# A graph network on one core: ScalarE's instructions tied to the order in which the kernel writes them

## Chip, core and metric

The kernel runs on one core of a Trainium2 chip. The metric is the time of one execution on the device in microseconds (us), the median of three runs. One further execution was recorded by the hardware profiler; all durations below come from its trace.

## What is computed

Three layers of a graph network (SAGE), each the sum of a node's own row and the mean of its neighbours' rows, through two weight matrices; then a residual and a layer norm; then one attention layer over the same edges, again with residual and layer norm. There are 12,500 nodes with 256 features, and 200,000 edges sorted by their target node.

```
def _sage_layer(x, src, dst, inv_deg, W_self, W_neigh, b):
    agg = jax.ops.segment_sum(x[src], dst, num_segments=N_NODES)
    mean = agg * inv_deg[:, None]
    return x @ W_self + mean @ W_neigh + b
...
h = jax.nn.relu(_sage_layer(features, ...)); h = jax.nn.relu(_sage_layer(h, ...)); h = _sage_layer(h, ...)
x = _layernorm(x + h)
x = _layernorm(x + attention(x))
```

## The kernel before

The neighbour sums of a layer are made in two ways at once. The edges of the lower nodes are taken in groups of 1,792 (14 columns of 128): layer 0 has 90 groups, layers 1 and 2 have 76 each. For each group GpSimd fetches 14 times 128 source rows (`gather`, line 121) into one of three buffers `xg`. From the middle of layer 0 on, ScalarE rounds the rows to a short format (line 858, tile `hl` or `win`), VectorE makes the rest (line 860), and TensorE multiplies them with a one-hot matrix of the targets into `pA` (lines 866, 869, 874). The nodes behind them (20 blocks of 128 in layer 0, 32 in the others) are summed densely: a matrix of edge counts in bytes, built in layer 0 (`form`, lines 615 to 652: VectorE makes two one-hots, TensorE multiplies them into `pc`, ScalarE packs `pc` into `win` at line 645), is multiplied with the whole table of rows (`sweeps`, lines 687 to 770). For each block of 128 table rows ScalarE turns a tile of counts into `c32` (line 749; 512 columns in layer 0, 1,024 in the others; three buffers), and TensorE runs four or eight matmuls of 128x512 on it (line 755). Such a block is called a sweep step here.

Each group also has an end. ScalarE copies half of the sum (`part`, line 904, then VectorE adds at 905) and scales it to `mean` (908); in layer 0 it copies the sum to `agg` (910). TensorE turns the rows (363) and makes eight weight products into `pO` (354). VectorE adds the bias in place (344). In layers 0 and 1 ScalarE then makes `hn` (346) and `hs` (659) with Relu; in layer 2 VectorE adds `x` (348) and takes statistics (334, 335), ScalarE takes the root `bn_rs` (337), and a later projection `zu` (376) is squared by ScalarE (`sq`, 672). The dense blocks end in the same way, with `own` (720), `hnd` (346) and `hs` (`end_block`, line 698).

The kernel's loop over groups (lines 928 to 957) writes the steps of three groups and of the sweeps in a fixed interleaving, `turns`. On TensorE that order is binding: `chained` ties the first matmul of each step behind the last one of the step before, without a semaphore. GpSimd's gathers are tied in the same way, and `hold_back` paces them. All other engines' orders are chosen when the kernel is built: a scheduler places an instruction where it expects its inputs to be there. On each engine the placed order is kept at run time.

Of the kernel before, what the change touches and what calls it, by code (L numbers as in the profile page):

```python
# [23 lines left out]
P = 128  # L24
# [15 lines left out]
CB = 7  # L40
# [8 lines left out]
def tile_gnn_resnorm(  # L49
# [70 lines left out]
    def gather(dst_ap, table, idx):  # L120
        return nc.gpsimd.indirect_dma_start(  # L121
            out=dst_ap, out_offset=None, in_=table,
            in_offset=bass.IndirectOffsetOnAxis(ap=idx, axis=0))


    src0 = const.tile([P, G0, GT], I32, name="src0")
# [61 lines left out]
    with tc.tile_pool(name="prep", bufs=1) as prep, \  # L188
# [126 lines left out]
        hex_ = prep.tile([KR, K], F32, name="hex_")  # L315
        nc.scalar.activation(hex_, hw, AF.Exp, bias=hmx)
        hsum = prep.tile([KR, 1], F32, name="hsum")
# [11 lines left out]
    def layernorm(wk, y, o):  # L329

        n = y.shape[0]
        st = wk.tile([n, nc.vector.BN_STATS_DIM], F32, name="bn_st")
        mv = wk.tile([n, nc.vector.BN_AGGR_DIM], F32, name="bn_mv")
        nc.vector.bn_stats(st, y)
        nc.vector.bn_aggr(mv, st)
        rs = wk.tile([n, 1], F32, name="bn_rs")
        nc.scalar.activation(rs, mv[:, 1:2], AF.Sqrt, bias=eps_t[:n])
        nc.vector.reciprocal(rs, rs)
        return nc.vector.tensor_scalar(o, y, mv[:, 0:1], rs, op0=OP.subtract, op1=OP.mult)

    def sage_end(wk, l, wts, po, hn, xb):

        n = po.shape[0]
        nc.vector.tensor_add(po, wts[2][:n], po)
        if l < L - 1:
            return nc.scalar.activation(hn, po, AF.Relu)
        y = wk.tile([n, D], F32, name="y")
        nc.vector.tensor_add(y, xb, po)
        return layernorm(wk, y, hn)
# [8 lines left out]
    def turned(wk, ps, tiles, name, bufs=None, by_act=False):  # L358
# [6 lines left out]
        if by_act:  # L365
            nc.scalar.activation(t, pt, AF.Copy)
        else:
            nc.vector.tensor_copy(t, pt)
# [28 lines left out]
    def attention_turned(wk, pt, n):  # L397
        agT = wk.tile([KR, n], F32, name="agT")
        nc.scalar.activation(agT, pt[:KR], AF.Copy)
        return agT  # L400

    def attention_end(wk, zz, pg):

        n = zz.shape[0]
        g = wk.tile([n, D], F32, name="g")
        nc.scalar.activation(g, pg, AF.Relu, bias=shrink[:n])
        nc.vector.tensor_add(g, zz, g)
        return g, layernorm(wk, g, g)
# [3 lines left out]

    DATA = mybir.DependencyReason.DATA
    AFTER = mybir.DependencyInfo(mybir.DependencyClass.NoSync, DATA)
    DONE = mybir.DependencyInfo(mybir.DependencyClass.Sync, DATA)
    loads = [None]
# [25 lines left out]
    def hold_back(first, then):  # L442

        tc.add_manual_dep(then.ins, first.ins.name, DONE, reason="the pace of the gathers")

    def after(first, then):

        tc.add_manual_dep(then.ins, first.ins.name, AFTER, reason="the order of the work")

# [21 lines left out]
    def fast_sage():  # L471
        with ExitStack() as fx:
# [7 lines left out]
            ones2 = wp.tile([P, 2], F32R, name="ones2")  # L480
            nc.scalar.activation(ones2, ones[:, :2], AF.Copy)
            invd = wp.tile([P, ND], F32, name="invd")
# [8 lines left out]
            for a in range(0, NG * GT, P):  # L491
# [3 lines left out]
                rt = wk.tile([P, P], F32, name="rt")  # L495
                nc.scalar.activation(rt[:m], pr[:m], AF.Copy)
                nc.sync.dma_start(rel_d[a:a + m, :], rt[:m])
# [10 lines left out]
            def split_x(pool, psum):  # L508
# [13 lines left out]
                for b in range(0, NQ, ZB):  # L522
# [5 lines left out]
                    for n, r in ((P, slice(0, m)), (N % P, slice(m, ZB))):  # L528
                        if r.start == r.stop:
                            continue  # L530
                        hi = hs[:n, r, :D]
                        nc.scalar.activation(hi.bitcast(F32R), xv[:n, r], AF.Copy)
                        nc.scalar.activation(ph[:n, r], hi, AF.Copy)
                        nc.vector.tensor_tensor(hs[:n, r, D:].bitcast(F32R), xv[:n, r], ph[:n, r], op=OP.subtract)
# [33 lines left out]
            def load_edges(pool, u):  # L568
# [41 lines left out]
                for i in range(3):  # L610
                    nc.tensor.transpose(pt[:, i], keys[:, i], ident)
                nc.scalar.activation(kt, pt, AF.Copy)
                held.append(kt)

            def form(pool, psum):
# [6 lines left out]
                for i, u in enumerate(parts):  # L622
# [3 lines left out]
                    for i0 in range(0, P, CP):  # L626
# [9 lines left out]
                        for c in range(0, CP, 2):  # L636
                            d = (i0 + c) * NC % P
                            if d == 0:
# [5 lines left out]
                            chained(*mm)  # L644
                            nc.scalar.activation(  # L645
                                win[:, :, d:d + 2 * NC].bitcast(U16).rearrange("p b (i t) -> p b i t", t=2),
# [8 lines left out]
            def finish(l, lk, bank, hn, po, last=False):  # L655

                if l < L - 1:
                    hs = lk.tile([P, 2 * D], F32R, name="hs", bufs=3)
                    nc.scalar.activation(hs[:, :D], po, AF.Relu)
                    hf = hs.bitcast(F32)  # L660
# [10 lines left out]
                sq = lk.tile([P, KR], F32, name="sq")  # L671
                nc.scalar.activation(sq, zu, AF.Square)
                nrm = lk.tile([P, K], F32, name="nrm")
# [13 lines left out]
            def sweeps(l, dk, dps, lk):  # L687
# [10 lines left out]
                def end_block(k, d, aggT, bank):  # L698
# [20 lines left out]
                    own = wk.tile([P, D], F32, name="own", bufs=1)  # L719
                    nc.scalar.activation(own, po, AF.Copy)  # L720
                    nc.vector.scalar_tensor_tensor(po, pn, invd[:, k + d:k + d + 1], own, op0=OP.mult, op1=OP.add)
# [16 lines left out]
                for k0 in range(ND - NDL[l], ND, sg):  # L738
                    assert all(k in whole for k in range(k0, k0 + sg))
                    px = [[dps.tile([P, 512], F32, name=f"px{f}{i}") for i in range(sc // 512)] for f in range(DC)]  # L740
                    for b in range(NQ):
# [6 lines left out]
                        c32 = dk.tile([P, sc], F32R, name="c32", bufs=3)  # L748
                        nc.scalar.activation(c32.rearrange("p (k d) -> p k d", d=P), c8[:, :, b % CB], AF.Copy)  # L749
                        made = []  # L750
# [14 lines left out]
                    for f in range(DC):  # L765
                        for i in range(sc // 512):
                            nc.scalar.activation(aggT[:, f, i * 512:(i + 1) * 512], px[f][i], AF.Copy)
                    left = end_sweep(k0, aggT, [ps])
# [30 lines left out]

            turn, H, summed = 0, GT // 2, []  # L800
            for l in range(L):
                table = x if l == 0 else hd[l - 1]
# [5 lines left out]
                with ExitStack() as lx:  # L808
# [11 lines left out]
                    def group(g):  # L820
# [28 lines left out]
                        for a in (0, H):  # L849
# [4 lines left out]
                            if halved:  # L854
                                hf = hi.bitcast(F32)
                                for j in range(0, H, 2):
                                    n = min(2, H - j)
                                    nc.scalar.activation(hi[:, b + j:b + j + n, :W], xg[:, a + j:a + j + n, :W], AF.Copy)  # L858
                                for j in range(H):
# [42 lines left out]
                        if l:  # L902
                            part = wk.tile([P, D], F32, name="part")
                            nc.scalar.activation(part, pa[:, D:], AF.Copy)
                            nc.vector.tensor_add(before[:, :D], part, pa[:, :D])
                        sums = before[:, :D] if l else pa[:, :D]
                        mean = wk.tile([P, D], F32, name="mean", bufs=3)
                        nc.scalar.activation(mean, sums, AF.Copy, scale=inv[:, g:g + 1])
                        if not l:
                            nc.scalar.activation(before[:, :W], pa[:, :W], AF.Copy)  # L910
                        yield
# [47 lines left out]
                    assert next(steps_, None) is None and (l or (next(forming, 0) == 0 and next(xsplit, 0) == 0))  # L959

            t1 = wp.tile([P, 1], F32, name="t1")
            nc.vector.reduce_max(t1, top, axis=AX.X)
# [6 lines left out]
    def fast_attention():  # L969
        loads[0] = None  # L970
        H = GT // 2
        with tc.tile_pool(name="att", bufs=2) as wk, \
# [11 lines left out]
            def group(g):  # L984
# [20 lines left out]
                oT = ohT[:, :T].rearrange("p j e -> p (j e)")  # L1005
                nc.scalar.activation(oT, rT, AF.Abs, bias=npidx)
                nc.scalar.activation(oT, rT, AF.Relu, scale=-1.0, bias=1.0)

                z2 = wk.tile([P, K, 2, R], F32R, name="z2", bufs=3)
                zk = zn.rearrange("p (k r) -> p k r", r=R)  # L1010
                nc.scalar.activation(z2[:, :, 0], zk, AF.Copy)
                nc.vector.tensor_tensor(z2[:, :, 1], zk, z2.bitcast(F32)[:, :, 0], op=OP.subtract)

                w = wk.tile([P, GT, 2 * AW], F32R, name="w", bufs=3)
                for a, n in ((0, H), (H, T - H)):
# [4 lines left out]
                          for j in range(n)]  # L1020
# [10 lines left out]
                    wf = wk.tile([P, H, AW], F32, name="wf")[:, :n]  # L1031
                    nc.scalar.activation(wf[:, :, KR:], lg, AF.Exp, scale=0.25)  # L1032
                    pe = pd[:, H * 2 * KR:H * 2 * KR + n * K].rearrange("p (t k) -> p t k", k=K)
                    nc.scalar.activation(pe, wf[:, :, KR:], AF.Copy)
                    nc.vector.tensor_mul(wf[:, :, :KR].rearrange("p t (k r) -> p t k r", r=R),  # L1035
                                         zs[:, a:a + n].rearrange("p t (k r) -> p t k r", r=R),
                                         pe.unsqueeze(3).to_broadcast([P, n, K, R]))
                    nc.scalar.activation(w[:, a:a + n, :AW], wf, AF.Copy)
                    nc.vector.tensor_tensor(w[:, a:a + n, AW:], wf, w.bitcast(F32)[:, a:a + n, :AW], op=OP.subtract)
# [9 lines left out]
                part = wk.tile([P, AW], F32, name="part")  # L1049
                nc.scalar.activation(part, pa[:, AW:2 * AW], AF.Copy)  # L1050
                acc = wk.tile([P, AW], F32, name="acc", bufs=3)
# [86 lines left out]
    def general_sage():  # L1138
        for l in range(L):
# [16 lines left out]
            with tc.tile_pool(name="gn", bufs=1) as wk, tc.tile_pool(name="gn_ps", bufs=1, space=PSUM) as ps:  # L1156
                wts = load_sage(wk, l)
                with tc.For_i(0, NBLK, 1) as i:
# [13 lines left out]
                    mean = wk.tile([NB, D], F32, name="mean")  # L1172
                    nc.scalar.activation(mean, ab[:, :D], AF.Copy, scale=iv)
                    po = sage_products(ps, wts, turned(wk, ps, [hb, mean], "hT")[0])[0]
# [12 lines left out]
    def general_attention():  # L1187
# [20 lines left out]
        with tc.tile_pool(name="gs", bufs=1) as wk, tc.tile_pool(name="gs_ps", bufs=1, space=PSUM) as ps:  # L1208
            with tc.For_i(0, NTE, 1) as i:
# [8 lines left out]
                w = wk.tile([TE, AW], F32, name="w")  # L1218
                nc.scalar.activation(w[:, KR:], lg, AF.Exp)
                nc.vector.tensor_mul(w[:, :KR].rearrange("p (k r) -> p k r", r=R),  # L1220
# [63 lines left out]
```

## Time and profile before

| | us |
|---|---|
| median of the three runs | 8058.46 |
| lowest and highest run | 8031.01 and 8086.6 |
| the profiled execution's own time | 6504.63 |
| its span, first to last instruction | 6502.8 |
| TensorE busy in the span | 5140.6 |
| GpSimd busy | 4809.5 |
| VectorE busy | 3906.3 |
| ScalarE busy | 3473.9 |

The first gather of layer 1 starts at 1705.5 us of the span, the first load that only layer 2 makes at 3105.2 us, and the attention's matmuls start at 4502.8 us. The layers thus take about 70 to 4480 us, and the attention some 2,020 us. The profiled execution is shorter than the runs by 1,554 us; no record of the runs says where they take longer. The mean granted clock of TensorE in the profiled execution is 0.815 of full speed. In the profile's rows PE is TensorE's matmuls, PEld its weight loads, DVE VectorE, ACT ScalarE, POOL GpSimd and SP the engine that issues most transfers.

### The profile page before, as it was taken

What the parts mean: (1) busy time and instruction counts of PE and PEld (TensorE: products, weight loads), DVE (VectorE), ACT (ScalarE), POOL (GpSimd) and SP (SyncE); (2) the same over time, 40 slices, a digit from 0 to 9 for tenths busy, and PEclk for the clock granted to TensorE, in tenths of its full rate; (3) what the DMA queues carried; (4) which work ended last, traced back from release to release, by engine and by line L of the source; (5) the groups of instructions that cost most, each with busy time, mean ns of one, the idle gap of its engine ahead of it and who ended that gap; (6) DMA issues with size and microseconds to landing.
All of it is one profiled execution on the core that took longest, in us unless ns stands there. A gap on an engine that the chain in (4) does not pass through costs nothing.

```text
span 6502.8 us, 86803 instructions
## 1 busy us (share of the span) xinstructions
PE 5140.6 (79%) x23570; PEld 4209.6 (65%) x23570; DVE 3906.3 (60%) x9939; ACT 3473.9 (53%) x6309; POOL 4809.5 (74%) x4977
## 2 busy tenths in 40 slices
PE   4789999888799999998899999995555555555555
PEld 3567777677577777786678888884444444444444
DVE  4867767555445555555456666665555655556555
ACT  2444555565466666664556666664454554545554
POOL 6767777777677777776777777776777777777775
PEclk8889999999899999998899999997555555555555
DMA  8978999898678888886788888885333333333332
GB/s 219 319 259 291 305 305 320 284 302 289 189 254 260 267 267 270 261 273 197 230 264 265 272 269 273 271 246 149 93 107 102 101 101 102 105 105 101 101 101 73
DMA packets 896774, 1391.65 MB, mean 214 GB/s; under 512 B 191216, under 2 KB 540424, under 8 KB 892173
## 3 DMA queue, kind: packets, MB, share of 16 engines
q1 hardware_dynamic: 650511, 834.50, 38.8%
q0 software_dynamic: 213152, 496.65, 26.9%
q10 hardware_dynamic: 32606, 54.81, 2.4%
q8 instruction: 189, 3.10, 0.2%
q14 instruction: 316, 2.59, 0.1%
HBM read 1175.15 MB, written 210.33 MB: 213 GB/s over the span
## 4 chain that ended last, share of the span: by engine, by line
PE 25%; POOL 10%; DMA 7%; DVE 5%; issue 5%; ACT 1%; DVEq 0%; POOLq 0%; SPq 0%; ACTq 0%
POOL zs L121 9%; PE px L755 9%; DMA zs<-zu_d,srcI 4%; PE pA L866 3%; DMA xg<-h_d,srcI 3%; PE pA L1042 3%; PE pD L1018 3%; PE pO L381 2%; PE pO L354 2%; PE pO L382 1%; DVE wf L1035 1%; DVE zz L1026 1%; DVE lg L1029 1%; PE pT L363 1%; PE pA L469 1%
## 5 line engine op out<-in xcount | busy, mean ns | idle before, releaser
L121 POOL DMA_INDIRECT xg<-h_d,srcI x2128 | 2076.2, 976 | 704.1 <-issue 288.6
L755 PE MATMUL px<-c,hz 128*128 128x512 f32 x8232 | 2255.5, 414 | 110.0 <-ACT c L749 83.5
L121 POOL DMA_INDIRECT zs<-zu_d,srcI x1563 | 1499.1, 959 | 505.5 <-issue 425.4
L755 PEld LDWEIGHTS px<-c,hz 128*128 128x128 f32 x8232 | 1521.7, 191 | 427.8 <-ACT c L749 107.1
L121 POOL DMA_INDIRECT xg<-in_x_dram,srcI x1218 | 1172.4, 963 | 426.9 <-issue 136.9
L749 ACT ACTIVATE c<-c 128x1024 fp32r<-128x1024 uint8 (+1 forms) x1274 | 1120.1, 892 | 598.7 <-PE px L755 424.3
L860 DVE TENSOR_TENSOR hl<-xg,hl 128x256 fp32r<-128x256 f32 x2128 | 790.1, 419 | 578.5 <-ACT hl L858 575.4
L858 ACT ACTIVATE hl<-xg 128x512 fp32r<-128x512 f32 x1216 | 648.6, 571 | 612.9 <-DMA xg<-h_d,srcI 484.5
L462 DVE TENSOR_TENSOR oh<-rel,gconst 128x1792 fp32r<-128x1792 f32 (+1 forms) x354 | 713.8, 2017 | 334.2 <-PE pA L866 193.1
L1056 PE MATMUL pT<-ident,ag 128*64 128x128 f32 x112 | 47.1, 421 | 887.5 <-DVE ag L392 887.5
L1056 PEld LDWEIGHTS pT<-ident,ag 128*64 128x64 f32 x112 | 14.4, 129 | 967.4 <-DVE ag L392 966.1
L1026 DVE TENSOR_TENSOR zz<-zs,pD 128x896 f32<-128x896 f32 x224 | 241.9, 1080 | 636.6 <-DMA zs<-zu_d,srcI 632.5
L866 PE MATMUL pA<-hl,oh 128*128 128x512 f32 x2128 | 574.7, 409 | 12.8 <-DVE hl L860 9.2
L866 PEld LDWEIGHTS pA<-hl,oh 128*128 128x128 f32 x2128 | 406.3, 193 | 108.5 <-DVE hl L860 13.8
L874 PE MATMUL pA<-xg,oh 128*128 128x258 f32 x1764 | 431.4, 397 | 6.1 <-ACT agg L910 3.4
L1018 PE MATMUL pD<-z,ohT 128*128 128x128 f32 x1563 | 360.7, 418 | 39.0 <-DVE wf L1035 21.9
L874 PEld LDWEIGHTS pA<-xg,oh 128*128 128x128 f32 x1764 | 343.7, 199 | 64.0 <-ACT agg L910 7.2
L645 ACT ACTIVATE win<-pc 128x392 uint16<-128x392 f32 x512 | 238.5, 494 | 272.3 <-PE pc L642 263.4
L1018 PEld LDWEIGHTS pD<-z,ohT 128*128 128x128 f32 x1563 | 346.8, 333 | 39.7 <-DVE wf L1035 22.2
L1042 PE MATMUL pA<-w,oh 128*128 128x136 f32 x1563 | 361.3, 418 | 0.0
L1032 ACT ACTIVATE wf<-lg 128x28 f32<-128x28 f32 x224 | 50.5, 226 | 576.4 <-DVE lg L1029 575.2
L634 DVE TENSOR_SCALAR ob<-iota,kt 128x196 bf16<-128x196 f16 x1024 | 349.7, 344 | 0.0
(257 smaller groups left out, 7879.8 us busy)
## 6 DMA issues: line engine op xcount, KB each, us to landing
hz<-hs_d SPq DMA_DIRECT2D x637, 512.0 KB
c<-cnt_d SPq DMA_DIRECT2D x112, 896.0 KB
ohT<-rel_d SPq DMA_DIRECT2D x111, 896.0 KB
hs_d<-hs SPq DMA_DIRECT2D x218, 256.0 KB
cnt_d<-win ACTq DMA_DIRECT2D x32, 1568.0 KB
xg<-h_d,srcI POOLq DMA_INDIRECT x2128
c<-cnt_d SPq DMA_DIRECT2D x70, 448.0 KB
zs<-zu_d,srcI POOLq DMA_INDIRECT x1563
```

The source lines that it names most:

```text
L121: return nc.gpsimd.indirect_dma_start(out=dst_ap, out_offset=None, in_=table, in_offset=bass.IndirectOffsetOnAxis(ap=idx, axis=0))
L462: nc.vector.tensor_tensor(oh[:, :m], r[:, :m].unsqueeze(2).to_broadcast([P, m, P]), nodes.unsqueeze(1).to_broadcast([P, m, P]), op=op)
L634: nc.vector.tensor_scalar(ob[:, c], iota16[:, 1:1 + NQ * 2], kt[:, 1, at], kt[:, 2, at], op0=OP.is_equal, op1=OP.mult)
L749: nc.scalar.activation(c32.rearrange("p (k d) -> p k d", d=P), c8[:, :, b % CB], AF.Copy)
L755: made.append(nc.tensor.matmul(px[f][i], hz[:, b % ZB, a:a + P].bitcast(F32R), c32[:, i * 512:(i + 1) * 512], start=b == 0 and part == 0, ...
L858: nc.scalar.activation(hi[:, b + j:b + j + n, :W], xg[:, a + j:a + j + n, :W], AF.Copy)
L860: nc.vector.tensor_tensor(lo[:, b + j, :D], xg[:, a + j, :D], hf[:, b + j, :D], op=OP.subtract)
L866: mm.append(nc.tensor.matmul(pa, oh[:, a + j], hl[:, j].rearrange("p i d -> p (i d)"), start=first, stop=stop))
L874: mm.append(nc.tensor.matmul(pa[:, :W], oh[:, a + j], xg[:, a + j, :W], start=first, stop=stop))
L1018: mm = [nc.tensor.matmul(pd[:, j * 2 * KR:(j + 1) * 2 * KR], ohT[:, a + j], z2.rearrange("p k i r -> p (k i r)"), start=True, stop=True) f ...
L1026: nc.vector.tensor_mul(zz, zg.unsqueeze(2).to_broadcast([P, n * K, 2, R]), pd[:, :n * 2 * KR].rearrange("p (m i r) -> p m i r", i=2, r=R))
L1042: mm = [nc.tensor.matmul(pa, oh[:, j], w[:, j], start=j == 0, stop=g == 0 and j == T - 1) for j in range(T)]
```

## The change

A wrapper `act` takes the place of `nc.scalar.activation` everywhere in the fast path. While a switch is on, which is from the first line of the loop over layers to its end, each activation is tied behind the one written ahead of it. The tie is the same that `chained` uses: a place in the engine's own order, with no semaphore. The transfers that ScalarE issues are not tied, nor are activations before the layers and in the attention. No instruction is added or taken away.

```
     DATA = mybir.DependencyReason.DATA
     AFTER = mybir.DependencyInfo(mybir.DependencyClass.NoSync, DATA)
     DONE = mybir.DependencyInfo(mybir.DependencyClass.Sync, DATA)

     def after(first, then):

         tc.add_manual_dep(then.ins, first.ins.name, AFTER, reason="the order of the work")

+    written = [False, None]
+
+    def act(*args, **kw):
+
+        i = nc.scalar.activation(*args, **kw)
+        if written[0]:
+            if written[1] is not None:
+                after(written[1], i)
+            written[1] = i
+        return i
...
-            return nc.scalar.activation(hn, po, AF.Relu)
+            return act(hn, po, AF.Relu)
...
-                        nc.scalar.activation(c32.rearrange("p (k d) -> p k d", d=P), c8[:, :, b % CB], AF.Copy)
+                        act(c32.rearrange("p (k d) -> p k d", d=P), c8[:, :, b % CB], AF.Copy)
...
             turn, H, summed = 0, GT // 2, []
+            written[0] = True
             for l in range(L):
...
+            written[0] = False
             t1 = wp.tile([P, 1], F32, name="t1")
```

The lines left out replace the other calls in the same way; `DATA`, `AFTER`, `DONE` and `after` only move up.

## Prediction

> **What bounds the kernel now.** I read the engines' totals first, then the stages, then the rows of single instructions, the waits and the timeline. First three stages (columns: busy us of PE, PEld, DVE, ACT, POOL, granted clock, DMA share, GB/s): the middle of layer 1, the start of layer 2, its middle; then two stretches of 20 us in layer 0.
>
> ```profile
> 2500.00:2900.00 400.00, 386.25 (x1727) 316.72 (x1726) 216.34 (x496) 258.79 (x434) 304.60 (x314) 0.99 0.83 267
> 3100.00:3500.00 400.00, 371.19 (x1669) 300.24 (x1669) 230.96 (x602) 232.73 (x385) 304.29 (x315) 0.97 0.81 254
> 3500.00:4000.00 500.00, 499.97 (x2381) 412.67 (x2380) 339.02 (x930) 307.26 (x525) 381.12 (x391) 1.00 0.87 271
> ...
> 600.00:620.00 20.00, 15.81 (x86) 11.78 (x85) 15.88 (x67) 8.36 (x20) 14.95 (x17) 0.91 0.80 260
> 1360.00:1380.00 20.00, 15.83 (x83) 12.85 (x82) 11.31 (x30) 12.59 (x28) 15.27 (x16) 0.99 0.88 292
> ```
>
> TensorE has no free time in layer 2's middle and 3 to 7% elsewhere in mid-layer. Summed over the stages from 70 to 4480 us it idles 369 us: 198 in the four stages that hold the starts and ends of layers, 172 in between. GpSimd is close behind: a gather takes 0.95 us and the pause after it 0.30, so 14 cost 17.5 us, against 18.0 to 18.4 us for a group (1,620 us / 90; 1,395 / 76; 1,380 / 76). ScalarE is busy for 60% only: its work doesn't matter, its places do.
>
> TensorE around a group's weight products in layer 2, and ScalarE at that time:
>
> ```profile
> 3806.74 1.03 PE L354 MATMUL pO<-ws,hT 128*128 128x256 f32 x4
> 3807.61 1.03 PE L354 MATMUL pO<-wn,hT 128*128 128x256 f32 x4
> 3808.29 2.19 PE L755 MATMUL px<-c,hz 128*128 128x512 f32 x8
> 3810.32 0.38 PE L363 MATMUL pT<-ident,hn 128*128 128x128 f32 x2
> 3810.45 2.09 PE L755 MATMUL px<-c,hz 128*128 128x512 f32 x8
> ```
> ```profile
> 3804.45 0.63 ACT L858 ACTIVATE hl<-xg 128x512 fp32r<-128x512 f32 x1 [0.51 <-PE pA L866]
> ...
> 3806.79 1.06 ACT L749 ACTIVATE c<-c 128x1024 fp32r<-128x1024 uint8 x1
> 3807.75 0.49 ACT L908 ACTIVATE mean<-agg,inv 128x256 f32<-128x256 f32 x1
> 3810.57 1.06 ACT L749 ACTIVATE c<-c 128x1024 fp32r<-128x1024 uint8 x1 [2.32 <-issue]
> 3811.53 0.28 ACT L337 ACTIVATE bn_rs<-bn_mv,eps_t 128x1 f32<-128x1 f32 x1
> ```
>
> TensorE goes from the products straight into the next sweep steps, since ScalarE had cast their counts (`c`) before it comes to the root (`bn_rs`) that depends on those products. Only few waits of TensorE on ScalarE are left (us in total, times, longest):
>
> ```profile
> PE px L755 <- ACT c L749: 83.5, 37, 6.9
> PE pc L642 <- ACT win L645: 47.7, 16, 17.6
> ...
> ACT hl L858 <- DMA xg<-h_d,srcI: 484.5, 293, 11.0
> ```
>
> **The change, part by part.** Nothing is added or removed; I compared the two built orders. In longest common order, 4180 of ScalarE's 6514 instructions keep their places, 21082 of TensorE's 22197, 5114 of GpSimd's 5127, 4609 of SP's 5016, 7820 of VectorE's 10126. So ScalarE changes, TensorE hardly, and VectorE follows ScalarE. Neither the gathers nor SP's loads move far (at most 28 and 40 places), and their number is the same; I cost them at nothing as GpSimd has no harder bound than before. If a load came late, a sweep step (2.0 us) waits for it.
>
> What matters is what stands behind an activation that waits. As written, a group's end reads: products on TensorE; `hn`, `hs` (or `bn_rs`) on ScalarE; then the next sweep step's cast and its matmuls. A layer 0 example from the new orders:
>
> ```
> ScalarE: hn_8051<-pO_8046, hs_8054<-pO_8046, c32_8064, win_7957<-pc_8070, c32_8074
> TensorE: pO_8046 (products), px<-c32_8064 (x4), pc_8070 (x2), px<-c32_8074 (x4)
> ```
>
> `c32_8064` cannot start before `hn` has had the products, and TensorE has nothing between the products and the matmuls that need `c32_8064`. I counted for each activation that waits on TensorE how much matmul time lies between what it waits for and the first matmul that needs it or anything behind it on ScalarE (0.25 us per 128x512 matmul, 0.22 per 128x256, as the rows above space them). For `hn` of the groups that cover is typically 3 or 8 us before (122 of 168), and below half a microsecond in 151 of 168 after. For the 108 `bn_rs` of layer 2 it is 5 us or more in 94 cases before, and below half a microsecond in 95 after. Each stall is the chain minus its cover:
>
> - `hn` and `hs`: VectorE's add 0.43 (line 344), `hn` and `hs` 0.26 and 0.27 from start to start, the cast 0.63 (512 columns) or 1.05 (1,024), three hand-overs of about 0.03 (2315.71 to 2315.74 is one): 1.7 us in layer 0, 2.1 in the others. 88 places in layer 0, mean 1.55 after cover: 137 us. 72 in layer 1, mean 2.11: 152 us.
> - Dense ends `own`, add, `hnd`, `hs`: 0.40 + 0.53 + 0.46 + 0.28 + 0.27 + the cast: 2.6 or 3.0 us and what stands between. 13 in layer 0, 41 us; 28 in layer 1, 97 us.
> - `win`: it waits for the pair of `pc` written just ahead, and the next cast stands behind it: 0.39 start to start + 0.63 + two hand-overs = 1.1 us. 186 places, 204 us.
> - `bn_rs`: add, add, statistics, aggregate 0.43 + 0.44 + 0.47 + 0.18, root 0.19 start to start, cast 1.05, hand-overs: 2.9 us. 106 places, mean 2.78: 294 us.
> - `sq`: copy 0.22, `sq` 0.24, cast 1.05 and hand-overs, 1.7 us; 81 places, 138 us.
> - All others, 30 us.
>
> The sum is 1,093 us: 385 in layer 0, 252 in layer 1, 456 in layer 2. The same count on the old order gives 44. What is late next is the whole TensorE chain, since matmuls keep their order; nothing gives the time back.
>
> Three terms the count leaves out. VectorE may be busy when a chain reaches it (54 to 75% in mid-layer; its usual piece is 0.42 us, its longest the one-hot of 2.0): some 390 chains by 0.25 us, 100 us; the ends are 0 and 390 x 2.0 = 780. TensorE's present idle in mid-layer, mostly late gathers, can hide stalls: 150 of the 172 us; the ends are 0 and all 369. Third, the clock. In my 20 us stretches, 18 with TensorE 70 to 79% busy had 0.85 on average, those above 90% had 0.99 to 1.00 (the two rows shown have 79%: 0.91 and 0.99). After the change TensorE would be 4,040 / 5,400 = 75% busy. By those rows, 3,860 us of matmul at full clock go from a mean clock of 0.956 to about 0.87: +400 us. [...] the gaps here are 1.1 to 3 us, [...] while the stretches of before with a low clock held longer ones (3.3 us at 601.8, 5.4 at 2309.9). [...] +50, and keep 400 for the range. [...]
>
> So 1,093 - 44 + 100 - 150 + 50 = about 1,050 us on the profiled execution, 6,505 to 7,550. The median of the runs is 1,554 us above that execution, and no row says why. Most stalls have no cover at all and don't depend on TensorE's speed, so I add them to the median: about 9,100 us.
>
> **Rivals.**
>
> - Hidden: in the timed runs something other than TensorE sets the pace. For it: gathers need 17.5 of 18.0 us even here; if the missing 1,554 us lie in the gathers, a group takes some 23 us, and TensorE with its stalls (16.7 + 4 to 6) fits in. Against it: nothing in the trace shows slower gathers. Then only starts and ends of layers pay: 100 to 300 us, about 8,250.
> - The clock falls with the busy share, as the rows have it or worse (0.80, the 60 to 69% rows): 3,860 / 0.80 - 4,040 = 785 us more, about 9,850. Against it are the short gaps.
> - Faster: in the old order casts of gathered rows (`hl`) stand ahead of sweep casts and block them when a gather is late (484.5 us of ScalarE's waits; TensorE idles 5.4 us at 2309.9 so). Written order puts them where TensorE needs them. All 369 us of idle recovered would give 7,690 if nothing stalled. It decides from the point where mean stalls are below 172 / 242 groups = 0.7 us per group; the count says 4.5.
> - That the order doesn't change: ruled out by 4180 of 6514.
>
> **How the numbers follow.** Chances: the stalls add up, 0.68; hidden, 0.17; clock, 0.11; faster, 0.04. The first case's own range is 8,740 (no VectorE delay, all idle used: +680) to 9,600 (clock +400 in place of 50, VectorE delay 250 in place of 100). The 8-in-10 range reaches into the hidden case below and the clock case above: 8,300 to 9,700. A measurement of this kernel can tell about 1% from no change. Faster by over 1%: 0.04; within 1%: 0.05, the best end of the hidden case; slower: 0.91.
>
> **What would show it.** In the profile after: waits of TensorE's `px` on `c` grow from 83.5 us and 37 times to several hundred us and hundreds of times; ScalarE's waits of `hn` on line 344 (105 us), `bn_rs` on line 335 (32 us), `sq` (17 us) and `win` on `pc` rise; TensorE's share in mid-layer falls to 75 to 80%; GpSimd's pauses grow, the attention keeps its 2,020 us. It is wrong if `px` seldom waits on `c`, if TensorE stays above 90%, or if the clock in mid-layer drops well below 0.9.

## The result and the profile after

| | kernel before, us | changed kernel, us | ratio (95% interval) |
|---|---|---|---|
| the runs that the forecast was made for | 8072.53 (8031.01 to 8110.42) | 9451.06 (9445.01 to 9469.82) | 1.1713 (1.1676 to 1.1751) |
| the same two kernels on another chip (run `after_again` below) | 6492.38 (6481.72 to 6495.36) | 7878.10 (7874.38 to 7884.78) | 1.2140 (1.2118 to 1.2161) |

The change makes the kernel slower, by 1,379 us in the first row and by 1,386 us in the second. The forecast was 9,100 us, within 8,300 to 9,700.

One thing has to be known to read what follows. The sets of runs fall into two kinds, by the chip, as far as five sets tell. In three of them the kernel before takes 7,964 to 8,073 us, in two, both on one chip, 6,492 us. The profiled execution of before (6504.63 us) is like the second kind, the profiled execution that came with the result like the first. I speak of the long chips and the short chip, and compare traces within a kind only: the shown profile of before with `after_again` (short), and the result's profile with `order_off`, which is the kernel before under another label (long). Length of each stage, and in it the time in which no matmul ran (for layer 2 up to the first matmul of the attention), from the traces in us; in the last column the matmul time in the layers that ran at a granted clock of 0.50:

| | layers 0, 1, 2 | TensorE idle in them | attention | matmul time at half clock, layers |
|---|---|---|---|---|
| before, short chip | 1636, 1400, 1385 | 209, 111, 70 | 2012 | 254 |
| changed, short chip | 2154, 1622, 2021 | 536, 260, 485 | 2009 | 967 |
| before, long chip | 2148, 1664, 1798 | 544, 290, 361 | 2276 | 871 |
| changed, long chip | 2556, 2174, 2350 | 846, 709, 750 | 2299 | 1531 |

The attention's program is the same in both kernels, and it keeps its time within a kind of chip. All of the loss is in the layers. The following views are of the changed kernel on the short chip. The engines' totals first (busy us, share of the span, instructions), then three stages as they were shown for before: the middle of layer 1, the start of layer 2, its middle (busy us of PE, PEld, DVE, ACT, POOL, granted clock, DMA share, GB/s).

```profile
PE 5623.4 (71%) x23570; PEld 4426.7 (56%) x23570; DVE 3995.3 (51%) x9939; ACT 3411.4 (43%) x6309; POOL 4778.9 (61%) x4977
```
```profile
2700.00:3100.00 400.00, 339.46 (x1405) 265.74 (x1404) 179.84 (x395) 197.56 (x343) 245.91 (x255) 0.95 0.69 216
3900.00:4300.00 400.00, 317.40 (x1327) 252.28 (x1326) 190.55 (x478) 176.10 (x300) 251.36 (x262) 0.93 0.66 202
4800.00:5300.00 500.00, 381.96 (x1548) 299.15 (x1546) 230.12 (x600) 196.59 (x347) 238.62 (x248) 0.89 0.58 175
```

TensorE was busy for 97, 93 and 100% of these stages; now it is busy for 85, 79 and 76%, at a clock of 0.95, 0.93 and 0.89 in place of 0.99, 0.97 and 1.00. GpSimd, which was close behind TensorE, now has 17 to 37% less work per microsecond. The waits (us in total, times, longest) point to the cause; in the kernel before, the first line was 83.5 us, 37 times, the last three 66.8 (46 times), 32.4 (22) and 424.3 us (372):

```profile
PE px L767 <- ACT c L138: 866.6, 492, 4.9
...
PE pc L654 <- ACT win L138: 57.6, 14, 14.1
...
ACT hl L138 <- DMA xg<-h_d,srcI: 50.0, 18, 11.2
...
ACT hn L138 <- DVE pO L363: 850.7, 159, 10.2
ACT bn_rs L138 <- DVE bn_mv L354: 554.7, 110, 10.2
...
ACT c L138 <- PE px L767: 10.2, 16, 3.3
```

All activations have line 138 now, that of the wrapper, and other lines are shifted by up to 19; each experiment below has line numbers of its own. The sweep's matmuls wait 492 times for the cast of their counts. The third line shows that ScalarE's waits for late gathers did fall, from 484.5 us to 50.0. The last line shows the casts' lead: before, a cast had to wait 372 times until TensorE had left a buffer, so it ran ahead of TensorE; now it has to 16 times.

One such wait in the timeline of the changed kernel, layer 2 (start, length; in brackets the idle time of the engine before it and what ended it):

```profile
4800.44 1.03 PE L373 MATMUL pO<-wn,hT 128*128 128x256 f32 x4
4801.51 0.43 DVE L363 TENSOR_TENSOR pO<-b,pO 128x256 f32<-128x256 f32 x1 [2.83 <-PE pO L373]
...
4803.10 0.29 ACT L138 ACTIVATE bn_rs<-bn_mv,eps_t 128x1 f32<-128x1 f32 x1 [8.25 <-DVE bn_mv L354]
4803.30 1.04 ACT L138 ACTIVATE c<-c 128x1024 fp32r<-128x1024 uint8 x1
...
4804.40 3.03 PE L767 MATMUL px<-c,hz 128*128 128x512 f32 x8 [2.93 <-ACT c L138]
```

The products end at 4801.47. VectorE's part of the layer norm takes until 4803.07, ScalarE has stood idle for 8.25 us in front of `bn_rs`, and only behind it comes the cast that TensorE needs: TensorE idles 2.93 us. (ScalarE kept its placed order throughout: in the records of before and of the result all 6,089 activations come in the order in which they were built.) The eight matmuls after it then take 3.03 us in place of 2.2. The clock shows why. These are four stretches of 3.41 us around that stall:

```profile
4798.50:4801.91 3.41, 2.97 (x14) 2.18 (x12) 0.58 (x2) 0.00 (x0) 2.50 (x4) 1.00 0.35 99
4801.91:4805.32 3.41, 0.93 (x4) 0.79 (x5) 2.05 (x7) 1.73 (x4) 0.43 (x1) 1.00 0.46 142
4805.32:4808.73 3.41, 3.41 (x12) 2.43 (x11) 0.76 (x2) 3.41 (x7) 0.00 (x0) 0.50 0.88 269
4808.73:4812.14 3.41, 3.41 (x16) 2.66 (x15) 2.50 (x7) 0.64 (x1) 2.13 (x3) 1.00 0.65 168
```

The second stretch has 0.93 us of matmuls, and the whole third one runs at a clock of 0.50, although TensorE is busy throughout; then the clock is full again.

### The profile page after: what moved, and what is told of

Same layout as the page of the kernel before. It is cut to its first block, busy times and chain, and to the rows that moved or that the text cites. A ratio compares the mean times of both kernels' runs of the same rounds, so it can differ in the third digit from the quotient of the medians.

```text
span 9448.6 us, 86747 instructions
## 1 busy us (share of the span) xinstructions
PE 5885.5 (62%) x23570; PEld 4628.9 (49%) x23570; DVE 3989.3 (42%) x9939; ACT 3417.0 (36%) x6309; POOL 4776.4 (51%) x4977
## 4 chain that ended last, share of the span: by engine, by line
PE 37%; DVE 12%; another core or an unknown queue 11%; issue 9%; ACT 4%; DMA 3%; POOL 2%; DVEq 0%; ACTq 0%; SPq 0%; POOLq 0%
PE px L767 16%; PE pA L879 5%; PE pD L1032 3%; PE pA L1056 3%; ACT c L138 3%; DMA zs<-zu_d,srcI 2%; POOL zs L121 2%; PE pO L400 2%; PE pO L401 2%; DVE zz L1040 2%; PE pO L373 2%; DVE oh L474 2%; DVE lg L1043 1%; DVE hl L873 1%
## 5 line engine op out<-in xcount | busy, mean ns | idle before, releaser
L767 PE MATMUL px<-c,hz 128*128 128x512 f32 x8232 | 2655.3, 471 | 1772.5 <-ACT c L138 1439.1
L767 PEld LDWEIGHTS px<-c,hz 128*128 128x128 f32 x8232 | 1794.7, 227 | 2331.0 <-ACT c L138 1571.2
L873 DVE TENSOR_TENSOR hl<-xg,hl 128x256 fp32r<-128x256 f32 x2128 | 749.9, 419 | 400.4 <-ACT hl L138 297.9
L879 PE MATMUL pA<-hl,oh 128*128 128x512 f32 x2128 | 633.8, 439 | 109.9 <-DVE hl L873 96.9
L138 ACT ACTIVATE hl<-xg 128x512 fp32r<-128x512 f32 x1216 | 597.3, 562 | 33.1 <-DMA xg<-h_d,srcI 30.2
L138 ACT ACTIVATE hn<-pO 128x256 f32<-128x256 f32 x166 | 63.6, 383 | 1455.6 <-DVE pO L363 1359.4
L887 PE MATMUL pA<-xg,oh 128*128 128x258 f32 x1764 | 496.3, 441 | 9.1 <-issue 5.7
L887 PEld LDWEIGHTS pA<-xg,oh 128*128 128x128 f32 x1764 | 395.4, 229 | 95.1 <-ACT agg L138 12.5
L645 DVE TENSOR_SCALAR oa<-iota,kt 128x128 bf16<-128x128 f16 x1024 | 260.8, 255 | 370.5 <-PE pc L654 268.6
L387 DVE COPY hT<-pT 128x512 f32<-128x512 f32 x235 | 161.9, 689 | 484.8 <-PE pT L382 235.3
```

The source lines that it names most:

```text
L138: i = nc.scalar.activation(*args, **kw)
L645: nc.vector.tensor_scalar(oa[:, c], iota16[:, :P], kt[:, 0, at], None, op0=OP.is_equal)
L767: made.append(nc.tensor.matmul(px[f][i], hz[:, b % ZB, a:a + P].bitcast(F32R), c32[:, i * 512:(i + 1) * 512], start=b == 0 and part == 0, ...
L873: nc.vector.tensor_tensor(lo[:, b + j, :D], xg[:, a + j, :D], hf[:, b + j, :D], op=OP.subtract)
L879: mm.append(nc.tensor.matmul(pa, oh[:, a + j], hl[:, j].rearrange("p i d -> p (i d)"), start=first, stop=stop))
L887: mm.append(nc.tensor.matmul(pa[:, :W], oh[:, a + j], xg[:, a + j, :W], start=first, stop=stop))
```

## Experiments

Twelve runs follow, of eleven kernels. Ratios are to the kernel before on the same chip.

| run | what is out of the written order | us | ratio (95% interval) | chip |
|---|---|---|---|---|
| order_off | all | 7960.53 | 0.9994 (0.9970 to 1.0018) | long |
| ends_free | group ends | 8659.59 | 1.0843 (1.0709 to 1.0976) | long |
| win_free | `win` | 9056.44 | 1.1339 (1.1203 to 1.1476) | long |
| ahead2_3 | none, casts written two steps earlier | 8696.88 | 1.0889 (1.0762 to 1.1017) | long |
| ends_win_free | group ends and `win` | 6533.75 | 1.0066 (1.0049 to 1.0083) | short |
| casts_free | sweep casts | 6575.10 | 1.0125 (1.0108 to 1.0142) | short |
| add_first | none, one-hot behind the bias add | 8025.26 | 1.2361 (1.2340 to 1.2381) | short |
| hl_free | casts of gathered rows | 7868.85 | 1.2117 (1.2097 to 1.2137) | short |
| after_again | none (the changed kernel) | 7878.10 | 1.2140 (1.2118 to 1.2161) | short |
| ahead2_3_again | none, casts written two steps earlier | 6599.42 | 1.0165 (1.0147 to 1.0183) | short |
| fill8 | none, more matmuls behind the products | 8613.18 | 1.3276 (1.3252 to 1.3299) | short |
| fill_apart | none, more matmuls in another bank | 9366.09 | 1.1727 (1.1677 to 1.1776) | long |

**The whole change undone.**

```
-            written[0] = True
+            written[0] = False
```

> The changed file with its switch never on, so the order of before. Both theories: within 1% of before, about 8,070 us. Its profile is the question: the profiled execution of before took 6,505 us where its runs took 8,070, the changed kernel's took what its runs took. If the records of this one show about 8,070 us, they tell what the runs of before wait for; if 6,505 again, that stays open.

7960.53 us beside 7964.33 for the kernel before: the wrapper itself costs nothing that shows. Its record, 7954.9 us long, is the before of the long chips in the table above.

**The changed kernel once more.** It ran unchanged beside two of the experiments, to have its time and its trace on the short chip.

> The changed kernel as it is, beside the others of this call; chips differ (before took 7,964 us beside the first experiments and 6,493 beside the last four). Theory (the stalls are lengths of chains and cost the same microseconds on any chip): before + 1,380 to 1,500, so 7,870 to 8,000 where before takes 6,493 (ratio 1.21 to 1.23), or 9,330 where before takes 7,964. Rival (the loss comes from the late completion signals of the chip with the long times): a ratio of 1.12 or less where before takes 6,493.

7878.10 us, a ratio of 1.2140: the loss is 1,386 us there too, although a bias add that waits for its products starts 0.04 us after they end (median of 180). The rival falls. Its trace is the changed kernel of the short chip in the tables and views above.

**Parts of the order undone.** In each of these, one condition in the wrapper leaves some activations out of the tie, by the tile that they write (`args[0]`) or read (`args[1]`); the comment names the run:

```
-        if written[0]:
+        if written[0] and not (str(args[0].tensor.name).startswith(('hn', 'hs', 'own', 'bn_rs', 'sq'))):    # ends_free
+        if written[0] and not (str(args[1].tensor.name).startswith('pc')):    # win_free
+        if written[0] and not (str(args[0].tensor.name).startswith(('hn', 'hs', 'own', 'bn_rs', 'sq', 'win'))):    # ends_win_free
+        if written[0] and not (str(args[0].tensor.name).startswith('c32') and str(args[1].tensor.name).startswith('c8')):    # casts_free
+        if written[0] and not (str(args[1].tensor.name).startswith('xg')):    # hl_free
```

> Tied as in the change, but not hn, hs, hnd, own, bn_rs and sq (the ends of groups and blocks), which the scheduler places. Theory (activations that wait for a product stand ahead of casts): the count of uncovered stalls falls from 1,093 to 340 us; the measured loss of 1,379 us is 1.31 times the 1,049 forecast, so (340 - 44) x 1.31 = 390 us remain: about 8,460 us, 8,250 to 8,650. Rival (the casts of gathered rows come too late and hold up GpSimd's gathers): these casts stay tied, so above 9,200 us.

> Tied as in the change, but not the packing of counts (win from pc, 512 of them in layer 0). Theory: the count falls from 1,093 to 897, so 9,450 - 196 x 1.31 = about 9,190 us (9,100 to 9,300), all of it in layer 0. Rival of late gathers: above 9,350 us.

On this chip the changed kernel would take 7,964.33 x 1.1713 = 9,328 us. With the ends free it is 669 us less, with `win` free 272 us less: 10 us beyond the upper end of the first expectation, and below the lower end of the second. Against the result's trace, of another set, that of `win_free` is 273 us shorter in layer 0, where `win` is made (2556 to 2283); layers 1 and 2 are 34 and 50 us shorter, and the kernel before takes 108 us less in the set of `win_free` than in that of the result. Both freed together was not run on a long chip; the two savings add up to 941 of the 1,364 us lost there.

> The group ends (hn, hs, hnd, own, bn_rs, sq) and win are taken out of the order at once; sweep casts, casts of gathered rows, part and mean stay in it. The count of uncovered waits falls to 119 us (before 44, after 1,093). Theory (a sweep cast queued behind an activation that waits for TensorE is the whole loss): close to before, 8,100 us, 8,000 to 8,250. If the two savings merely add as the single runs had them (9,328 - 668 - 272): 8,390. Rival (the other tied activations, casts of gathered rows first, cost time of their own): above 8,500.

> Only the sweep casts leave the order; every other activation keeps it. Count of uncovered waits: 194 us. Theory (it matters only that the sweep casts stand behind the waiting ones): 8,150 us, 8,000 to 8,350. Rival (VectorE's order, which has a one-hot of 2.0 us within four places ahead of the bias add in 172 of 373 places here, 174 in the changed kernel, 9 in the kernel before, delays the products' chain with or without a queue on ScalarE): 8,600 or more.

Both ran on the short chip, where the changed kernel takes 1,386 us more than the one before. With ends and `win` free 41 us of that are left, with only the sweep casts free 83 us. The expected figures were for a long chip; as ratios they were 1.017 and 1.023, and the measured 1.0066 and 1.0125 are lower still. (In `ends_win_free` the name `win` also takes in the 216 casts of gathered rows in layer 0 that write a tile of that name; `hl_free` below bears on these.) So on the short chip nearly the whole loss goes away from either side: take the waiting activations out of the queue, or take the casts out from behind them. `casts_free` still has the one-hot ahead of the bias add in 172 places, so VectorE's new order costs next to nothing once the casts stand free: the rival falls. In `ends_win_free` TensorE's wait on the casts is back to what it was before:

```profile
PE px L767 <- ACT c L138: 56.9, 35, 6.6
```

> The casts of gathered rows leave the order, everything else keeps it. Count of uncovered waits: 994 us. Theory: 9,328 - 100 = 9,230, 9,150 to 9,340. Rival (the loss is ScalarE waiting at a cast of gathered rows for a late gather, with sweep casts and group ends behind it): below 8,800.

7868.85 against 7878.10 us for the changed kernel, where 100 us less were expected; the intervals of the two ratios overlap, so no cost of the casts of gathered rows shows. Late gathers are not the cause of the loss.

**The same order, with the casts written earlier.** The order stays fully tied, but the loop of the sweep writes each cast two steps ahead of the matmuls that use it, into the same three buffers; the load of the bytes that a cast reads moves up with it:

```
+                    for b in range(AHEAD):        # AHEAD = 2
+                        cast(b)
                     for b in range(NQ):
...
-                        c32 = dk.tile([P, sc], F32R, name="c32", bufs=3)
-                        act(c32.rearrange("p (k d) -> p k d", d=P), c8[:, :, b % CB], AF.Copy)
+                        if b + AHEAD < NQ:
+                            cast(b + AHEAD)
+                        c32 = ahead_.pop(0)
```

> Fully tied, but the kernel writes each cast of a sweep step two steps ahead of its matmuls, in the same three buffers. Theory: the tie itself costs nothing, what is written is what matters; the count falls to 172 us, so 8,070 + (172 - 44) x 1.31 = about 8,240 us (8,000 to 8,500). Rival of late gathers: the casts of gathered rows now stand behind two more casts, so no better than the change, above 9,300 us.

> The changed kernel with every sweep cast written two steps ahead, once more, for a chip where before takes 6,493 us. Count of uncovered waits 172 us. Theory (two steps, 4 us, cover a chain where the signal of the products comes at once, and not where it comes some 4 us late): ratio to before 1.02 to 1.05 where before takes 6,493; 1.09 again where before takes 7,964. Rival (the count misses what the order costs, on any chip): 1.08 or more on both.

On the long chip the first expectation failed: 8,697 us, not 8,240. On the short chip the kernel takes 6,599 us, 107 us more than before, a little below what was expected. There the order costs almost nothing once the casts stand two steps ahead, so it is not the fixed order that costs but where the casts stood in it. Why two steps weren't enough on the long chip one place in its timeline shows (layer 1):

```profile
2641.89 1.03 PE L375 MATMUL pO<-wn,hT 128*128 128x256 f32 x4
2642.56 3.99 PE L778 MATMUL px<-c,hz 128*128 128x512 f32 x16
...
2645.78 2.02 DVE L476 TENSOR_TENSOR oh<-rel,gconst 128x1792 fp32r<-128x1792 f32 x1 [6.47 <-PE px L778]
...
2650.11 0.43 DVE L365 TENSOR_TENSOR pO<-b,pO 128x256 f32<-128x256 f32 x1 [1.25 <-remote]
...
2652.22 2.93 PE L778 MATMUL px<-c,hz 128*128 128x512 f32 x6 [5.67 <-ACT c L140]
```

The products end at 2642.92, TensorE works through the two prepared steps until 2646.55, but VectorE stands idle for 6.47 us in front of a one-hot and adds the bias, which comes behind it, only at 2650.11. The chain is 9 us long, the cover 4 us.

**The one-hot of VectorE.** The changed kernel as it is, and on VectorE one tie more, which puts the one-hot of a group behind an earlier group's bias add:

```
                         oh = onehot(wk, nodes, srel, F32R if halved else F32)
+                        if len(adds) > 1:
+                            after(adds[-2], ohs[0])
```

> The whole order as changed, and on VectorE the one-hot of a group is put behind the bias add of the group two earlier, so that a one-hot stands within four places ahead of that add in 32 places, not 174. Theory (the long stalls of 8 to 12 us hold a one-hot of 2.0 us): about 85 such stalls and some 90 shorter ones lose 2 us each, 9,328 - 300 = 9,030, between 8,900 and 9,180; the stalls of 8 to 12 us move to 6 to 8. Rival (the one-hot runs while the signal of the products is still late, so its time is hidden): 9,330 within 50.

A miss in sign: 8025.26 us, 147 more than the changed kernel. The timeline of this run in layer 2:

```profile
4917.26 0.43 DVE L364 TENSOR_TENSOR pO<-b,pO 128x256 f32<-128x256 f32 x1 [1.35 <-PE pO L374]
4917.59 2.01 DVE L475 TENSOR_TENSOR oh<-rel,gconst 128x1792 fp32r<-128x1792 f32 x1
...
4919.53 0.41 DVE L368 TENSOR_TENSOR y<-xb,pO 128x256 f32<-128x256 f32 x1
```

The one-hot now stands right behind the bias add, in the middle of the layer norm that `bn_rs` waits for. The 71 stalls behind `bn_rs` that I find in the trace grow from a mean of 2.86 us to 4.55; those behind `hs` stay (1.91 and 1.89). Layer 2 takes 187 us more and layer 1 30 us more, while layer 0, which has no layer norm, takes 68 us less, with 238 us of matmuls at half clock in place of 400. On the short chip the one-hot ahead of the add did little harm, as `casts_free` shows. Whether it does on a long chip was not tried.

**Does the clock follow the short stalls?** Both runs give TensorE work behind every group's products that nobody reads:

```
+            def filled(hT, w, n):
+                mm = [nc.tensor.matmul(spare, hT[:, i % (2 * DC)], w[i % (2 * DC) // DC][:, i % DC],
+                                       start=True, stop=True) for i in range(n)]
+                chained(mm[0], mm[-1])
...
                         chained(*mm)
+                        filled(hT, wts[l], 8)              # fill8: spare is the other half of pO's bank
+                        filled(hT, wts[l], (3, 4, 5)[l])   # fill_apart: spare is a tile of pT
```

> The changed kernel with eight more 128x256 matmuls (about 2.0 us) on TensorE behind the products of every group, written to a spare part of the bank and read by nobody, so that TensorE has work where it would stall. Theory [...]: the half-clock time in the layers falls by 40% or more and the kernel is 100 to 350 us faster than the changed kernel on the same chip, although it does some 610 us more of matmuls at full clock. Rival (the clock doesn't follow short stalls): 128x512 matmuls as long as before and the time 0 to 250 us longer than the changed kernel's.

This run did not test what it was made for. Its timeline:

```profile
2521.58 1.03 PE L577 MATMUL pO<-wn,hT 128*128 128x256 f32 x4
2522.64 0.43 DVE L365 TENSOR_TENSOR pO<-b,pO 128x256 f32<-128x256 f32 x1 [5.25 <-PE pO L577]
...
2524.76 4.34 PE L776 MATMUL px<-c,hz 128*128 128x512 f32 x16 [2.16 <-ACT c L140]
```

The bias add waits for the last added matmul (line 577), since that writes the same tile, so each stall stays as long as it was (2.16 us) and is only pushed back: 1,257 us of idle time, against 1,281. Each fill also takes 3.1 us, not 2.0, because each of the eight products is two instructions in the record (3,872 for 242 groups): 747 us of matmuls more, and 735 us more time. Neither expectation is met. One thing it does show: in layer 0 TensorE idles as long as before (520 and 536 us), but 199 us of its matmuls run at half clock, not 400. So the total of idle time alone does not set the clock; how it lies in time might (see the last section).

> The fill once more, now in the bank of pT, so that the bias add behind the products doesn't wait for it: 3, 4 and 5 more 128x256 matmuls per group in layers 0, 1 and 2 (1.5, 2.05 and 2.6 us, about the length of the stall there, 500 us in all), read by nobody. The changed kernel takes 7,878 us where before takes 6,492. Theory [...]: idle time in the layers falls from 1,240 to about 800 us, half-clock time from 1,160 to about 500, and the kernel takes 7,500 to 7,750 us (ratio to before 1.155 to 1.195). Rival (the clock doesn't follow the short stalls): half-clock time stays above 1,000 us and the kernel takes 7,880 to 8,000 (ratio 1.214 or more).

This one ran on a long chip, with a ratio of 1.1727 against 1.1713 for the changed kernel. Against the result's trace it has 398 us more of matmul time, 424 us less idle time (1,881 against 2,305), and 338 us less time at half clock (2,133 against 2,471). So the added matmuls cost nothing that shows, and the half-clock time fell with the idle time, but by 14% and not by more than half: on a long chip many stalls outlast the fill (1.5 to 2.6 us against a mean of 5.6 behind `hs` there). Neither expectation is met, and the clock's part is not shown by an experiment of its own.

## Why the prediction was right, and which term was off

**The mechanism and the places.** The forecast said that activations waiting for TensorE would stand ahead of the next sweep cast. `casts_free` and `ends_win_free` show that this is the loss on the short chip: 83 and 41 us remain of 1,386. The signs came as written down: `px` waits for `c` 492 times, ScalarE's waits of `hn` and `hnd` for the bias add rose from 105 to 904 us, of `bn_rs` from 32 to 555, of `sq` from 17 to 457, of `win` on `pc` from 263 to 845, and TensorE is busy for 74 to 85% in mid-layer, against 75 to 80 forecast. One sign of being wrong came in part: the clock is 0.87 to 0.96 in most of mid-layer, but lower in the middle of layer 0, here before and after the change:

```profile
800.00:1240.00 440.00, 411.33 (x2110) 327.55 (x2109) 288.96 (x1108) 221.46 (x495) 327.28 (x343) 0.97 0.89 302
```
```profile
800.00:1240.00 440.00, 327.01 (x1363) 237.86 (x1362) 194.90 (x737) 136.89 (x305) 202.58 (x214) 0.83 0.57 184
```

**The length of the stalls.** On the short chip, the stalls over 0.3 us that a cast ended, by the activation that stood ahead of that cast on ScalarE:

| ahead of the cast | forecast: places, mean us | found: places, mean us |
|---|---|---|
| `hn`, `hs` of groups and dense ends | 201, 2.1 | 147, 1.91 |
| `bn_rs` | 106, 2.8 | 71, 2.86 |
| `win` | 186, 1.1 | 172, 1.16 |
| `sq` | 81, 1.7 | 63, 1.59 |

The chain lengths are right within a tenth or so. The places are fewer. Another 25 stalls have `mean`, `aggT` or `agg` between; where the rest went was not traced. All 478 stalls add up to 863 us. The largest other wait of TensorE that grew was no part of the forecast: its sums (`pA`) wait 104.6 us for VectorE's half of the gathered rows, 9.2 before.

**The sum.** Less the 150 us that present idle time would absorb, plus 100 for VectorE, the count came to 999 us. TensorE's idle time grew by 891 us (327, 149 and 415 in the layers, against 385, 252 and 456 in the raw count): right within about a tenth. Layer 1 is over-counted most. The VectorE term by itself was not needed: the chain of `hs` was 1.91 us, not longer than the 2.1 us of the sum. One reading was off: the forecast gave TensorE 3 to 7% of free time in mid-layer outside layer 2's middle, but from 1240 to 1700 us it idles 14% (394.3 us busy of 460); its total of 172 us has this in it.

**The clock: the term that was off.** The forecast took +50 us, an estimate of mine from the short gaps, and kept the +400 of the rows for the range. On the short chip 967 us of matmuls ran at half clock, against 254 before. At half clock 128x512 matmuls start 0.43 us apart, at full clock 0.23, so 46% of the difference is the cost by this estimate: 713 x 0.46 = 328 us. On the long chips the same working gives (1531 - 871) x 0.46 = 304 us. The rows of 20 us, which paired 75% busy with a clock of 0.87, were near; my estimate from the short gaps was not. Here, in 80% of the 223 places where the clock fell in the layers, no gap in the 10.3 us ahead was over 3.4 us long, one step of the grid in the last section; in the kernel before, from which the forecast judged, 29 of 54 had such a gap.

Matmul time grew by 482 us in all, so 154 us are left beside the clock. The last matmul ahead of a gap lasts 0.39 us in the record where otherwise the next starts after 0.23, and there are 523 more gaps over 0.3 us; that makes some 85 us, and the rest is open. Added up: 891 + 482 - 3 in the attention = 1,370, and the two profiled spans differ by 7874.8 - 6502.8 = 1,372. That is 322 us above the 1,050 of the forecast: idle time is 108 us below its 999, matmul time 432 above its 50, and some 280 of these are the clock.

**The base.** The forecast added the stalls to the median of 8,058 us, not knowing why the profiled execution was 1,554 us shorter. The reason was the chip. Adding was right in the total (1,379 us on a long chip, 1,386 on the short one), but its reason, that the stalls are as long on any chip, was not, and that the totals agree so well is partly luck. On a long chip idle time grew by 302 + 420 + 389 = 1,111 us and matmul time by 359; these two traces are of two sets, whose kernels before differ by 108 us. The stalls behind `hs` and `bn_rs` last 5.6 and 5.1 us there, not 2 to 3, while layer 0 of before already had 544 us of idle time, into which part of them may have fallen.

**The rivals.** *Hidden* (8,250): no; GpSimd's gathers gave way: its idle time in the layers grew from 1,129 to 2,484 us on the short chip. *The clock falls with the busy share* (9,850): the clock did fall, at some 330 us in place of 785. *Faster*: the waits for late gathers fell from 484.5 to 50.0 us as it said, but TensorE's idle time more than tripled; and no more than the 390 us that it idled before could be won there.

## What to carry to other kernels

An in-order engine that prepares operands for another must have each preparation queued ahead of whatever waits for that other engine; count for each waiting instruction how much work the other engine has left when it gets there. If the order is to be fixed, write the preparation early enough first (here two steps: 1.0165 in place of 1.2140), with cover for the longest chain that any chip shows and not for the one in the profile. Here TensorE's stalls cost about a third more than their length through the clock (some 330 us beside 891), so leave room for that in a forecast.

## What the runs showed of the hardware

**In these records the clock of TensorE changed at steps of 3.41 us.** In the layers, all 108 changes in the record of before and all 669 in that of the result lie within 0.02 us of a grid of 3.41 us. I sorted the stretches of `after_again` on its grid by how much of each TensorE was idle, and by the clock of the stretch that followed:

| idle share of a stretch | full clock, then full | full, then half | half, then full | half, then half |
|---|---|---|---|---|
| below 10% | 666 | 0 | 198 | 0 |
| 10 to 20% | 95 | 0 | 24 | 5 |
| 20 to 40% | 213 | 1 | 0 | 71 |
| 40 to 50% | 121 | 13 | 0 | 11 |
| 50 to 60% | 31 | 63 | 0 | 7 |
| over 60% | 0 | 146 | 0 | 32 |

Of the stretches at full clock, none of the 761 that were idle for less than 20% was followed by one at half clock, but 63 of the 94 that were idle for 50 to 60%, and all 146 that were idle for more. Of those at half clock, 222 of the 227 that were idle for less than 20% were followed by one at full clock, and none of the other 121. The records of before and of the result look the same: at full clock and over 60% idle, 44 of 44 and 261 of 261 were followed by half clock, below 20% none of 450 and none of 393. From these counts I estimate that a stall of 2.9 us, as of `bn_rs`, is enough by itself if most of it falls in one stretch (85% of 3.41), and that each stretch at half clock then costs up to 1.6 us (46% of 3.41); one of 1.2 us, as of `win` (35%), is enough only if others lie close by. That it is the idle time that sets the clock is read from the order of events in the records; the runs that were to force it did not settle it.

**On the long chips VectorE goes on late behind TensorE.** The result's trace, a long chip, layer 1:

```profile
2989.74 1.03 PE L373 MATMUL pO<-wn,hT 128*128 128x256 f32 x4
2995.29 2.02 DVE L474 TENSOR_TENSOR oh<-rel,gconst 128x1792 fp32r<-128x1792 f32 x1 [10.67 <-remote]
...
2997.43 0.42 DVE L363 TENSOR_TENSOR pO<-b,pO 128x256 f32<-128x256 f32 x1
...
2999.53 5.90 PE L767 MATMUL px<-c,hz 128*128 128x512 f32 x16 [8.77 <-ACT c L138]
```

The products end at 2990.77 and VectorE, idle for 10.67 us, goes on 4.5 us later; in the place shown for the short chip it went on after 0.04 us. It takes the one-hot first, whose buffer an earlier sum on TensorE had to leave, and TensorE idles 8.77 us. Such places are common: of the 306 bias adds in a trace, nine in ten start within 1.5 us of the end of their products on the short chip, but within 8.0 us on the long one (before the change 2.9 and 9.6), whatever stands ahead of them on VectorE included. The attention, whose program is the same, shows what the kind of chip alone does; a stretch of it on the short chip, and one on a long chip, both of the changed kernel:

```profile
5900.00:7800.00 1900.00, 1028.13 (x3940) 865.20 (x3941) 1125.81 (x2127) 953.90 (x1598) 1441.32 (x1506) 0.50 0.34 102
```
```profile
7200.00:9400.00 2200.00, 1039.08 (x3975) 873.09 (x3975) 1136.62 (x2148) 953.86 (x1611) 1450.90 (x1514) 0.50 0.29 89
```

Nearly as many instructions with nearly the same busy times on every engine (within 1.1%) take 1,900 us on the short chip and 2,200 on the long one: it is the time between them that is longer. What delays VectorE stays open. The records of the long chips also hold only 46,000 to 61,000 semaphore events, where those of the short chip hold some 146,000, so many releasers in them are missing ("remote", "issue"); whether that has the same cause was not tried.
